# Cross-attention with a state-space scan on one core: pair-wise value products, projections in pieces, statistics and sums on ScalarE

## The chip, the core and the metric

The kernel runs on one core of one Trainium2 chip. The metric is the device time of one execution in microseconds; lower is better. The kernel before takes 2643.56 us, the median of 3 runs (2635.56 to 2644.17).

A core has five engines with a queue each, worked off in order: TensorE (PE: matmuls and transposes; its weight loads are shown as PEld), VectorE (DVE), ScalarE (ACT), GpSimd (POOL) and SyncE (SP), which here does nothing but issue transfers. An instruction that waits for another engine holds up all that is queued behind it.

## What is computed

The layer has 4096 queries of width 512 (`x`), 3202 keys and values that come from a second sequence, and 8 heads of 64. Cut to what matters here:

```python
xn   = layernorm(x, g1, beta1);  cn = layernorm(ctx, g1, beta1)
q    = xn @ Wq.T + bq;  k, v = cn @ Wk.T + bk, cn @ Wv.T + bv     # in 8 heads
attn = softmax(q @ k.T / 8)                                       # over 3202 keys
x1   = x + (attn @ v) @ W_o.T + b_o
U    = (layernorm(x1, g2, beta2) @ W_in.T + b_in) @ Bmat          # 4096 x 64
s_t  = silu(s_(t-1) @ A.T) + U_t                                  # a scan over the 4096 rows
out  = x1 + states @ Cmat + mod                                   # mod: one row, from ctxb
```

All of it is float32. The softmax takes a true maximum over the keys.

## The kernel before

**Stages.** A first stage (to 263 us of the profile) normalizes the 3202 rows of `ctx`, makes keys and values for all heads, parks them in DRAM (`kd`, `vd`), and makes the queries of the first chunk. The main loop (263 to some 2497 us) is the attention. A last stage projects the last chunk, runs the scan as three sweeps over 128-column blocks, and writes the output.

**The main loop.** The queries are cut into 8 *chunks* of 512 (`Q`). For each chunk the loop runs over 4 pairs of heads (`hp`) and 2 halves of 256 queries: that is a *unit*, 8 units to a chunk and 64 in all. A unit has 13 *steps*; a step handles two blocks of some 124 keys (so 2 heads x 2 key blocks x 256 queries, a tile of 123 x 1024). Each step of the loop carries five operations on tiles that belong to different steps of work, a software pipeline written out by hand (line 718, `manual_schedule`: what the program issues first stands first in each queue):

- `scores` (L453): four matmuls into the PSUM tile `s` (two such tiles exist), then the *copy* on ACT to SBUF (L469).
- `running` (L471), one step later: DVE takes the running maximum `top` from `s` (L480). The tile `s` is free again after this and the copy.
- `subtract` (L512), 16 steps after the scores: DVE takes the maximum off the copy (L514), in place.
- `weights` (L521), 17 steps after: ACT does the exponential in place (L524), POOL adds it to the sum `acc` (L533).
- `product` (L535), 18 steps after: four matmuls with the values into `po` (L542).

A `scores` matmul contracts 64 rows, a `product` matmul fills 64 output columns, all others use the whole 128 x 128 array.

**At the end of a unit** come the maximum over the keys (`maximum`, L482: eight transposes `tt` of `top`, two reductions on DVE, four transposes that spread the result, `mb`) and, after its last product, `finish` (L578: `both` on POOL, four transposes `pd`, a reduction `rd` and a reciprocal on DVE, the copy `wide` on ACT, two transposes `rb`, and the division on DVE, L613).

**Beside it** run two queues of generators, `first` (finish) and `rest`: `queries(Q + 1)` (L147) makes the next chunk's queries and `project(Q - 1)` (L616) takes the chunk before through the output projection `pa`, the second normalization, the transposes `tp` and the projection `pu` into `u`. `background` (L704) advances each by one `yield` at the end of a step, so after the copy of that step's scores in ACT's queue. A projection is issued whole: the 16 matmul passes of `pq` or the 8 of `pa` stand together.

**Transfers.** `load_k` and `load_v` (L674, L683) fetch keys and values once for both halves of a unit pair, into 13 buffers each. All main-loop transfers are in SP's queue: keys, values, the rows `x` for both generators, and the store of `x1` (L648), which waits for DVE's sum.

**The last chunk's projection** (L786) runs four generators in turn outside the hand-written order. Its PSUM tiles come from `ps_m` (2 banks), and its sum tile `x1` has one buffer. Between its operations POOL adds `modb` to 32 row tiles (`fetch`, L778).

Of the kernel before, what the change touches and what calls it, by code (L numbers as in the profile page):

```python
# [18 lines left out]
P = 128  # L19
# [26 lines left out]
def xattn_ssm_kernel(  # L46
# [58 lines left out]
    ln = actx.enter_context(tc.tile_pool(name="ln", bufs=2))  # L105
# [25 lines left out]

    def transposes(pool, tag, xh, n, name):

        tp = pool.tile([P, NC, P], F32, tag=tag, name=f"tp_{name}")
        for c in range(NC):
            nc.tensor.transpose(  # L136
                tp[:, c, :n], xh[:n, c * P : (c + 1) * P], ident[:n, :n]
            )
        return tp[:, :, :n]

    xp_ = actx.enter_context(tc.tile_pool(name="xp", bufs=2))
    xnp = actx.enter_context(tc.tile_pool(name="xnp", bufs=2))
    qp = actx.enter_context(tc.tile_pool(name="qp", bufs=6))
    ps_m = actx.enter_context(tc.tile_pool(name="ps_m", bufs=2, space=PSUM))
    qt = {}

    def queries(Q, fetched=None):  # L147

        xns = []
        for half in range(2):  # L150
            xn = xnp.tile([P, NC, QU], F32, tag="xn", name=f"xn_{Q}_{half}")
            xns.append(xn)
            for t in range(NT // 2):
                r = Q * QB + half * QU + t * P
                if fetched:
                    xt = fetched[:, half * (NT // 2) + t, :]
                else:
                    xt = xp_.tile([P, H], F32, tag="x", name=f"x_{r}", bufs=3)
                    nc.sync.dma_start(xt, x[r : r + P, :])
                    yield False  # L160
                scaled = normalize(xt, P, f"x{r}", later=True)
                yield False
                yield False
                xh = scaled()
                yield False
                tp = transposes(ps_m, "m", xh, P, f"x{r}")
                yield True
                nc.scalar.copy(xn[:, :, t * P : (t + 1) * P], tp)
                yield False
                yield False  # L170
        for hp in range(NC):
            pq = ps_m.tile([P, 512], F32, tag="m", name=f"pq_{Q}_{hp}")
            for half in range(2):
                for i in range(NC):
                    nc.tensor.matmul(  # L175
                        pq[:, half * QU : (half + 1) * QU],
                        wq[:, i, hp * P : (hp + 1) * P],
                        xns[half][:, i, :],
                        start=(i == 0),
                        stop=(i == NC - 1),  # L180
                    )
            yield True
# [5 lines left out]
            yield False  # L188
# [22 lines left out]
    def shift(k):  # L211

        pr = ps_m.tile([P, 512], F32, tag="m", name=f"pr_{k}")
# [9 lines left out]
        pb = ps_m.tile([P, 512], F32, tag="m", name=f"pb_{k}")  # L223
# [15 lines left out]
    def side():  # L239
# [30 lines left out]
        pw = ps_m.tile([P, 512], F32, tag="m", name="pw")  # L270
# [8 lines left out]
        pt = ps_m.tile([P, NC, P], F32, tag="m", name="pt")  # L279
# [12 lines left out]
        pb = ps_m.tile([P, 512], F32, tag="m", name="pb")  # L292
# [16 lines left out]
        pm = ps_m.tile([P, 512], F32, tag="m", name="pm")  # L309
# [11 lines left out]
        for dst, terms in (  # L321
# [3 lines left out]
            pr = ps_m.tile([P, 512], F32, tag="m", name="pr")  # L325
# [122 lines left out]
    sp_ = lctx.enter_context(tc.tile_pool(name="sp_", bufs=NDC + LAG + 4))  # L448
# [3 lines left out]
    def scores(w, c):  # L452
# [3 lines left out]
        for b in range(2):  # L456
            for a in range(2):
# [3 lines left out]
                    kts[(*w["at"][:2], c)][r, b * n : (b + 1) * n],  # L461
# [20 lines left out]
    def maximum(w):  # L482

        m = small.tile([P, 2, 2], F32, tag="m", name=f"m_{w['name']}")
        tps = []
        for t in range(2):
            tp = ps_m.tile([P, 2, 2, CK], F32, tag="m", name=f"tt_{w['name']}_{t}")
            tps.append(tp)
# [7 lines left out]
        yield  # L496
        for t in range(2):
            nc.vector.tensor_reduce(  # L498
                m[:, t, :], tps[t].rearrange("p a b k -> p a (b k)"), AX.X, ALU.max
            )  # L500
        yield
        mb = ps_b.tile([P, 2, QU], F32, tag="b", name=f"mb_{w['name']}")
        w["mb"] = mb
        for t in range(2):
            for a in range(2):
# [4 lines left out]
                )  # L510

# [456 lines left out]
```

## Time and profile before

| | |
|---|---|
| time, median of 3 runs | 2643.56 us |
| the profiled execution, its time | 2643.8 us |
| the profiled execution, its span | 2642.0 us |
| first stage | 0 to 263 us |
| main loop: first scores to last scores | 263.3 to 2465.4 us |
| last products, projection of the last chunk, scan | 2465.4 to 2642 us |

The span is what lies between the first and the last instruction; 1.8 us lie around it.

The timeline gives the start of every scores instruction. Each unit has 13 groups of them, so the start of each unit can be read off, and with it how long it lasts. The chunks 2 to 7 repeat one pattern to 0.4 us:

| unit of the chunk | 1 | 2 | 3 | 4 | 5 | 6 | 7 | 8 | sum |
|---|---|---|---|---|---|---|---|---|---|
| chunk 2 to 5, us | 30.9 | 34.8 | 38.2 | 36.0 | 32.3 | 32.7 | 44.9 | 30.9 | 280.8 |
| chunk 1, us | 24.3 | 27.8 | 30.9 | 32.8 | 32.7 | 44.9 | 30.9 | 30.9 | 255.3 |
| chunk 8, us | 30.9 | 34.8 | 38.2 | 36.0 | 30.8 | 30.9 | 30.9 | | |

Units 2 to 4 of a chunk carry `project`, units 5 and 6 the normalization in `queries`, unit 7 its four projections `pq`; units 1 and 8 have nothing beside them but `finish`. In chunk 1 there is nothing to project and `queries` comes a unit earlier.

In a line of the profile, a group such as `L480 DVE TENSOR_TENSOR top<-s,top` names line, engine, operation, and output and inputs. A timeline line gives start, duration, engine, line, operation, tiles, shape and count, and in brackets the idle time before it and what ended it. Neighbouring instructions of one engine overlap by some 0.05 to 0.1 us, so what one costs in a full queue is the distance from its start to the next start, not its duration.

### The profile page before, as it was taken

What the parts mean: (1) busy time and instruction counts of PE and PEld (TensorE: products, weight loads), DVE (VectorE), ACT (ScalarE), POOL (GpSimd) and SP (SyncE); (2) the same over time, 40 slices, a digit from 0 to 9 for tenths busy, and PEclk for the clock granted to TensorE, in tenths of its full rate; (3) what the DMA queues carried; (4) which work ended last, traced back from release to release, by engine and by line L of the source; (5) the groups of instructions that cost most, each with busy time, mean ns of one, the idle gap of its engine ahead of it and who ended that gap; (6) DMA issues with size and microseconds to landing.
All of it is one profiled execution on the core that took longest, in us unless ns stands there. A gap on an engine that the chain in (4) does not pass through costs nothing.

```text
span 2642.0 us, 44166 instructions
## 1 busy us (share of the span) xinstructions
PE 2498.9 (95%) x16588; PEld 1422.2 (54%) x16588; DVE 2144.1 (81%) x2320; ACT 1837.8 (70%) x2085; POOL 2066.3 (78%) x1170
## 2 busy tenths in 40 slices
PE   7989899999999999999999999999999999999857
PEld 3445456555565555555655555555655555555433
DVE  2210897999979897999799988999799979999725
ACT  2232787877878787878787777778787878788510
POOL 1020497998979997999799988989799979999860
PEclk9999999999999999999999999999999999999966
DMA  3422221112212121222112211222121312221133
GB/s 124 138 87 73 74 68 49 51 57 84 59 45 62 50 83 32 58 65 68 45 54 68 67 56 51 57 84 59 43 62 49 86 30 60 64 58 54 60 112 128
DMA packets 164458, 176.62 MB, mean 67 GB/s; under 512 B 13480, under 2 KB 137424, under 8 KB 164242
## 3 DMA queue, kind: packets, MB, share of 16 engines
q1 hardware_dynamic: 155070, 157.68, 20.6%
q10 hardware_dynamic: 9172, 16.06, 1.8%
q8 instruction: 134, 2.20, 0.4%
q14 instruction: 82, 0.67, 0.1%
HBM read 143.81 MB, written 29.89 MB: 66 GB/s over the span
## 4 chain that ended last, share of the span: by engine, by line
PE 50%; DVE 27%; issue 11%; ACT 7%; POOL 2%; DMA 1%; SPq 1%; ACTq 0%; DVEq 0%; POOLq 0%
DVE top L480 17%; PE s L459 14%; PE po L542 12%; DVE p L514 5%; PE pq L175 4%; ACT p L469 4%; PE pa L627 4%; PE pv L388 3%; PE pk L414 3%; ACT p L524 2%; PE tt L491 2%; PE py_c L870 1%; DVE rd L599 1%; PE mb L506 1%; PE pu L659 1%
## 5 line engine op out<-in xcount | busy, mean ns | idle before, releaser
L533 POOL TENSOR_TENSOR acc<-p,acc 123x1024 f32<-123x1024 f32 x698 | 1658.7, 2376 | 112.2 <-ACT p L524 70.6
L469 ACT COPY p<-s 123x1024 f32<-123x1024 f32 (+1 forms) x832 | 834.9, 1004 | 274.6 <-PE s L459 261.9
L514 DVE TENSOR_TENSOR p<-p,mb 123x1024 f32<-123x1024 f32 (+1 forms) x832 | 1000.0, 1209 | 0.8 <-PE mb L506 0.8
L459 PE MATMUL s<-q,k 64*123 64x256 f32 (+1 forms) x6656 | 941.4, 402 | 61.2 <-DVE top L480 49.4
L524 ACT ACTIVATE p<-p 123x1024 f32<-123x1024 f32 (+1 forms) x832 | 880.2, 1058 | 141.2 <-DVE p L514 134.0
L480 DVE TENSOR_TENSOR top<-s,top 123x1024 f32<-123x1024 f32 x704 | 855.9, 1216 | 140.1 <-ACT p L469 132.2
L542 PE MATMUL po<-p,v 123*64 123x256 f32 (+1 forms) x6656 | 900.4, 392 | 1.1 <-ACT o L585 0.9
L459 PEld LDWEIGHTS s<-q,k 64*123 64x123 f32 (+1 forms) x6656 | 560.2, 182 | 374.3 <-DVE top L480 169.3
L542 PEld LDWEIGHTS po<-p,v 123*64 123x64 f32 (+1 forms) x6656 | 404.4, 136 | 399.0 <-issue 222.5
L533 POOL TENSOR_TENSOR acc<-p,p 124x1024 f32<-124x1024 f32 x64 | 152.0, 2376 | 161.2 <-ACT p L524 161.0
L627 PE MATMUL pa<-wo,o 128*128 128x512 f32 x256 | 119.6, 612 | 2.5 <-DVE x L636 2.5
L115 POOL TENSOR_SCALAR ve_c<-mv_c 123x1 f32<-123x1 f32 (+1 forms) x26 | 5.9, 228 | 146.9 <-DVE mv_c L113 116.7
L175 PE MATMUL pq<-xn,wq 128*128 128x256 f32 x512 | 117.9, 383 | 0.0
L358 DVE COPY ct<-tp_c 128x492 f32<-128x492 f32 (+1 forms) x13 | 8.7, 671 | 127.8 <-PE tp_c L136 127.8
L480 DVE TENSOR_TENSOR top<-s,p 124x1024 f32<-124x1024 f32 x64 | 77.7, 1214 | 38.7 <-DMA k<-kd 37.4
L175 PEld LDWEIGHTS pq<-xn,wq 128*128 128x128 f32 x512 | 94.8, 190 | 20.5 <-issue 6.3
L388 PE MATMUL pv<-wv,ct 128*123 128x512 f32 (+1 forms) x208 | 97.8, 615 | 0.0
L422 ACT ACTIVATE ks<-pk,bias 128x492 f32<-128x492 f32 (+2 forms) x28 | 18.0, 643 | 111.8 <-PE pk L414 63.6
L414 PE MATMUL pk<-ct,wk 128*128 128x492 f32 (+2 forms) x224 | 89.2, 550 | 0.0
L588 POOL TENSOR_TENSOR both<-acc 124x512 f32<-124x512 f32 x63 | 80.8, 1283 | 4.9
L627 PEld LDWEIGHTS pa<-wo,o 128*128 128x128 f32 x256 | 46.8, 192 | 62.5 <-issue 56.5
L498 DVE TENSOR_REDUCE m<-tt 128x2 f32<-128x496 f32 x128 | 79.7, 662 | 0.7 <-PE tt L491 0.7
(158 smaller groups left out, 1345.5 us busy)
## 6 DMA issues: line engine op xcount, KB each, us to landing
k<-kd SPq DMA_DIRECT2D x352, 123.0 KB
v<-vd SPq DMA_DIRECT2D x352, 123.0 KB
xr<-in_x_dram SPq DMA_DIRECT2D x32, 256.0 KB
out_dram<-row_c ACTq DMA_DIRECT2D x32, 256.0 KB
k<-kd SPq DMA_DIRECT2D x64, 124.0 KB
v<-vd SPq DMA_DIRECT2D x64, 124.0 KB
x<-in_x_dram SPq DMA_DIRECT2D x28, 256.0 KB
x1d<-x SPq DMA_DIRECT2D x28, 256.0 KB
```

What stands on the lines that cost most here:

```text
L175: nc.tensor.matmul(pq[:, half * QU : (half + 1) * QU], wq[:, i, hp * P : (hp + 1) * P], xns[half][:, i, :], start=(i == 0), stop=(i == NC ...
L388: nc.tensor.matmul(pv[:n, :H], ct[:, i, o : o + n], wv[:, i, :], start=(i == 0), stop=(i == NC - 1),)
L414: nc.tensor.matmul(pk[:, :n_g], wk[:, i, hp * P : (hp + 1) * P], ct[:, i, :n_g], start=(i == 0), stop=(i == NC - 1),)
L459: nc.tensor.matmul(s[:n, a, b, :], kts[(*w["at"][:2], c)][r, b * n : (b + 1) * n], q[r], start=True, stop=True,)
L469: nc.scalar.copy(t[:n], s[:n])
L480: nc.vector.tensor_tensor(w["top"][:n], s[:n], before[:n], ALU.max)
L514: nc.vector.tensor_tensor(t[:n], t[:n], w["mb"][:n].unsqueeze(2).to_broadcast([n, 2, 2, QU]), ALU.subtract,)
L524: nc.scalar.activation(t[:n], t[:n], AF.Exp)
L533: nc.gpsimd.tensor_tensor(w["acc"][:n], t[:n], before[:n], ALU.add)
L542: nc.tensor.matmul(w["po"][a * HD : (a + 1) * HD, 0, :], vts[(*w["at"][:2], c)][:n, b, a * HD : (a + 1) * HD], t[:n, a, b, :], start=(c == ...
L588: nc.gpsimd.tensor_tensor(both, acc[:, :, 0, :], acc[:, :, 1, :], ALU.add)
L627: nc.tensor.matmul(pa, o_t[Q, c][:, t * P : (t + 1) * P], wo[:, c, :], start=(c == 0), stop=(c == NC - 1),)
```

## The change

The change keeps every result and shifts work between engines and within the step order:

- **Products by pairs.** At an odd step of a unit the products of this step and of the one before are issued together; at an even one none (the 13th stands alone).
- **Projections in pieces.** `pq` and `pa` are issued one matmul (of 512 columns) at a time, one per step. The two banks are split: `ps_m` for projections, `ps_f` for maxima and finish.
- **Maxima over two steps.** The transposes `tt` are issued in two halves at the ends of two steps, each followed by its reduction.
- **Statistics on ScalarE.** In the main loop `normalized` replaces the DVE statistics: a pass of ACT with a row sum, POOL's mean, a second pass of ACT (square) with a row sum, POOL's root, and the scaling as before.
- **Sums on ScalarE.** `rd` is made by four ACT instructions with a row sum; `u` is biased by ACT.
- **Order.** The "head" parts of the generators now stand in the step between `weights` and `scores` (before: after `scores`); the matmul parts ("pe") at its end, one per step, and none in the three steps after a unit's end. The projection runs as two generators `a` and `b`, two tiles each.
- **Keys and values per unit.** They are fetched for each half anew, into 6 and 9 buffers; `sp_` has one more.
- **The last chunk's projection** gets five banks of its own (`ps_t`), its matmuls alternate between the four tiles, and its emission order changes with the generator.

```diff
+    def normalized(xt, name, got):
+        xh = ln.tile([P, H], F32, tag="xh", name=f"xh_{name}")
+        total = ln.tile([P, 1], F32, tag="total", name=f"total_{name}")
+        nc.scalar.activation(xh, xt, AF.Identity, accum_out=total)
+        yield "head"
...
+        nc.gpsimd.tensor_scalar(mean, total, -1.0 / H, None, ALU.mult)
+        yield "head"
+        yield "head"
...
+        nc.scalar.activation(xh, xt, AF.Square, bias=mean, accum_out=square)
+        yield "head"
...
+        nc.gpsimd.tensor_scalar(ve, square, 1.0 / H, EPS, ALU.mult, ALU.add)
...
+        nc.gpsimd.tensor_tensor(rstd, ve, neg_half, ALU.pow)
...
+        nc.gpsimd.tensor_tensor(nmr, mean, rstd, ALU.mult)
+        yield "head"
+        yield "head"
+        nc.scalar.activation(xh, xt, AF.Identity, bias=nmr, scale=rstd)
+        got.append(xh)
...
-    ps_m = actx.enter_context(tc.tile_pool(name="ps_m", bufs=2, space=PSUM))
+    ps_m = actx.enter_context(tc.tile_pool(name="ps_m", bufs=1, space=PSUM))
+    ps_f = actx.enter_context(tc.tile_pool(name="ps_f", bufs=1, space=PSUM))
...
+            for i in range(NC):
+                nc.tensor.matmul(
+                    pq,
+                    wq[:, i, hp * P : (hp + 1) * P],
+                    xn[:, i, :],
...
+                if i < NC - 1 and not fetched:
+                    yield "pe"
+            yield "head"
...
-    sp_ = lctx.enter_context(tc.tile_pool(name="sp_", bufs=NDC + LAG + 4))
+    sp_ = lctx.enter_context(tc.tile_pool(name="sp_", bufs=NDC + LAG + 5))
...
         for t in range(2):
-            tp = ps_m.tile([P, 2, 2, CK], F32, tag="m", name=f"tt_{w['name']}_{t}")
-            tps.append(tp)
+            tp = ps_f.tile([P, 2, 2, CK], F32, tag="m", name=f"tt_{w['name']}_{t}")
...
-        yield
-        for t in range(2):
+            yield
             nc.vector.tensor_reduce(
...
-        nc.vector.tensor_reduce(rd, pd, AX.X, ALU.add)
...
+        for t in range(2):
+            for a in range(2):
+                nc.scalar.activation(
+                    junk, pd[:, t, a, :], AF.Identity, accum_out=rd[:, t, a : a + 1]
+                )
+        yield "head"
         nc.vector.reciprocal(rd, rd)
         nc.scalar.copy(wide, rd.unsqueeze(3).to_broadcast([P, 2, 2, HD]))
...
             for c in range(NC):
                 nc.tensor.matmul(
                     pa,
...
+                if c < NC - 1:
+                    yield "pe"
+            yield "head"
             x1 = xp.tile([P, H], F32, tag="x1", name=f"x1_{r}")
             nc.vector.tensor_tensor(x1, pa, xt, ALU.add)
...
+                got = []
+                yield "head"
+                nc.sync.dma_start(x1d[r : r + P, :], x1)
+                yield from normalized(x1, f"y{r}", got)
...
-            nc.vector.tensor_scalar(
+            nc.scalar.activation(
                 u[hs, :, c0 : c0 + P // L].rearrange("s j c -> s c j"),
...
-        if half == 0:
-            t = kp.tile([P, 2 * CK], F32, tag="k", name=f"k_{Q}_{hp}_{c}")
+        t = kp.tile([P, 2 * CK], F32, tag="k", name=f"k_{i}_{c}", bufs=AHEAD + 2)
...
+        t = kp.tile([CK, 2, P], F32, tag="v", name=f"v_{i}_{c}", bufs=AHEAD + 5)
...
+    beside = {"finish": [], "a": [], "b": [], "queries": []}
...
+    def heads():
+        for k in beside:
+            if advance(k, "head") and owner == [k]:
+                owner.clear()
+
+    def tail():
+
+        if advance("finish", "pe"):
+            return
+        for k in owner or ("a", "b", "queries"):
+            if advance(k, "pe"):
+                owner[:] = [k]
+                break
...
             if prev:
                 running(*prev)
+            for k in (2, 3):
+                if k in ends:
+                    next(ends[k]["max"])
             if exp:
                 weights(*exp)
+            heads()
             if now:
                 scores(*now)
...
-                product(*mul)
+
+                w, c = mul
+                for k in (c - 1, c) if c % 2 else (c,) if c == NDC - 1 else ():
+                    product(w, k)
...
-            background(more=1 not in ends)
...
+            if not ends:
+                tail()
...
-    tails = [project(NQB - 1, (t,), (tp_, NT, NT)) for t in range(NT)]
+    lastx = ExitStack()
+    ps_t = lastx.enter_context(tc.tile_pool(name="ps_t", bufs=5, space=PSUM))
+    tails = [project(NQB - 1, (t,), (tp_, NT, NT, ps_t)) for t in range(NT)]
```

## The prediction

> **What bounds the kernel now.** I read the stages first, then the timeline of a light unit and of a heavy one, then groups, waits and the tail. 83% of the span is the main loop, so the stretch from 340 to 2480 us comes first:
>
> ```profile
> core 0: us, PE busy (x) PEld busy (x) DVE busy (x) ACT busy (x) POOL busy (x), PEclk, DMA share, GB/s
> 340.00:2480.00 2140.00, 2086.36 (x15018) 1210.44 (x15014) 1971.02 (x2017) 1688.65 (x1863) 1925.08 (x998) 1.00 0.20 58
> ```
>
> The reader is to see that three engines are above 89%, that ACT has 451 us free, that the granted clock is 1.00 throughout and that the transfers use a fifth of their engines. None of them bounds the loop alone, so each unit must be summed. I take pitches (start to next start) from stretches without gaps:
>
> ```profile
> 880.70 1.13 PE L459 MATMUL s<-q,k 64*123 64x256 f32 x8
> 881.76 1.08 PE L542 MATMUL po<-p,v 124*64 124x256 f32 x8
> 882.78 0.66 PE L136 MATMUL tp_y<-ident,xh_y 128*128 128x128 f32 x4
> 883.36 0.91 PE L459 MATMUL s<-q,k 64*123 64x256 f32 x6
> ```
>
> Scores cost PE 1.06, products 1.015, `tp` .585; read likewise, `tt` .996, `mb` and `pd` .57 each, `rb` .37, `pu` .97, a `pq` block 3.65 and a `pa` block 3.63. DVE: `top` 1.135, subtraction 1.128, `m` .58, `rd` .70, the reciprocal .10, division .33, `bn_stats` with its second step .81, `x1` .725, `u` .275. A unit has 12 `top`s and 13 subtractions, so DVE needs 12x1.135 + 13x1.128 + 2x.58 + .70 + .10 + .33 = 30.6; PE needs 29.5 in a light unit (1 and 8 of a chunk), and such a unit lasts 30.9. Over the eight units PE's sums are 29.5 34.7 38.3 36.2 30.7 30.7 44.1 29.5 (273.6). The larger of PE's and DVE's sum gives every unit within .9 us. So light units, and 5 and 6, are DVE's; 2, 3, 4 and 7 are PE's.
>
> What matters most for this change is how tight the loop is in a light unit:
>
> ```profile
> 2434.33 1.21 DVE L514 TENSOR_TENSOR p<-p,mb 123x1024 f32<-123x1024 f32 x1
> 2435.46 1.22 DVE L480 TENSOR_TENSOR top<-s,top 123x1024 f32<-123x1024 f32 x1
> 2435.57 1.06 ACT L524 ACTIVATE p<-p 123x1024 f32<-123x1024 f32 x1 [0.30 <-DVE p L514]
> 2436.54 0.99 ACT L469 COPY p<-s 123x1024 f32<-123x1024 f32 x1
> 2437.72 1.22 DVE L480 TENSOR_TENSOR top<-s,top 123x1024 f32<-123x1024 f32 x1
> ```
>
> The exponential starts .03 after its subtraction ends, the copy follows at 2436.54 and ends at 2437.53, and `top` of the same scores starts .19 later. In all 768 pairs of the trace `top` never starts before the copy ends (least distance .03 us). So there is a ring: subtraction 1.2, exponential .96, copy 1.0, then `top`; anything put into ACT between exponential and copy beyond .19 us holds DVE up. Today the small ACT work stands behind the copy, where the next exponential has .30 us to wait anyway.
>
> **What the change removes and adds, part by part.**
>
> *Products by pairs.* Going from scores to products costs PE more than staying: two product blocks in one run, from the end of the loop, show it.
>
> ```profile
> 2487.34 1.90 PE L542 MATMUL po<-p,v 123*64 123x256 f32 x16
> 2489.07 1.03 PE L558 MATMUL pd<-p,ones 123*64 123x256 f32 x8
> ```
>
> 1.73 for two, against 2.03. A unit has six pairs and so saves six switches of about .15: .9 per unit, 7.3 per chunk; two scores that come to stand together save another .1, 1 per chunk. This is PE time, worth something only in PE's units. A pair delays the next scores by .85; the second tile of `s` takes that up.
>
> *Pieces.* A piece is two passes of .429 and one switch of .197: 1.055. Four make 4.22 against 3.63: +.59; eight blocks per chunk: +4.7. What it removes is the hole of a whole block:
>
> ```profile
> 734.64 1.23 DVE L480 TENSOR_TENSOR top<-s,top 123x1024 f32<-123x1024 f32 x1 [3.39 <-ACT p L469]
> ...
> 734.93 3.62 PE L175 MATMUL pq<-xn,wq 128*128 128x256 f32 x16
> ```
>
> DVE stood for 3.39 us around such blocks. But in units 2 to 4 and 7 PE has no gap there, so closing DVE's hole alone gives nothing; the gain comes from moving: `pq` now falls on units 7 and 8 with two blocks each, so PE has 37.0 + 37.0 where it had 44.1 + 29.5, and unit 8 no longer idles PE. The two units lasted 75.8 and should last 74.2: −1.6.
>
> The Trainium skill ("Perfetto Trace Analysis", Optimizing Tensor Performance, on matmuls) says that larger matmuls are more efficient than smaller ones. By that alone the pieces would just cost their 4.7 us per chunk; the row of the 3.39 us hole says that a block costs its neighbours as well.
>
> *Maxima.* `tt` in two halves: one more switch, +.17 per unit, 1.3 per chunk on PE. PE's sums thereby become 28.4 33.8 36.0 36.5 32.3 29.6 37.0 37.0 = 270.6, −3.0 per chunk.
>
> *Statistics.* DVE loses .81 for each of 8 tiles per chunk, 6.5 us, mostly in units 1 to 5. ACT gains two passes of 128x512 per tile. The scaling beside them has a pitch of .72; with a row sum I bound each by .72 and 1.06 (the exponential with twice the columns) and take .75, the nearest row. All three now stand between exponential and copy, so each loses .56 net of the .19 where DVE or ACT sets the pace. POOL gets `mean` (.3) per tile: 262 us per chunk, below every estimate of a chunk here.
>
> *Sums.* `rd` leaves DVE (−.70 per unit: 29.9) for four ACT instructions on 128x124, all in one step. The nearest rows: a copy of 128x128 from PSUM by ACT is .28, `wide` .40. Four are 1.1 to 2.0 with the writes to one scratch tile in turn; I take 1.5, of which 1.3 is lost after the slack. `wide` then waits for a reciprocal that stands behind other DVE work: +.2. The biased `u` is .3 on ACT, .1 lost; it takes .275 from DVE.
>
> The Trainium skill ("ScalarE: Activation LUTs", Rules for kernel authors) puts plain arithmetic on VectorE, not on ScalarE. Its formula in the section on what ACT_TABLE_LOAD costs (186 ns and .833 ns per element) makes four times 289 ns, 1.16 us, an estimate; the light unit would be .3 shorter by it, 31.4. It speaks against this part either way, and the row that bears on it is `rd` at .70 on DVE for all four sums.
>
> *Light unit after:* 29.9 + .3 (as now, 30.9 against 30.6) + 1.3 + .2 = **31.7** (31.3 to 32.2 by the bounds of `rd`), against 30.9. So a unit of the kind that DVE binds gets .8 longer although DVE has less to do.
>
> *Heavy units.* For each I set PE's sum beside the ring (30.2 + 1.5 + .56 per pass + `x1` .725 + .3 to .4 per `xn` or `q`). Passes per unit, from the built order: 0 1 9 5 5 4 0 0.
> Unit 2: PE 33.8, ring 33.0; only four steps carry a piece and the others fall back to the ring's pace, so 34.8. Unit 3: PE 36.0, ring 38.7; several passes share a step and pay the slack in the shadow of a piece: middle, 37.5. Unit 4: 36.5 and 34.9: 36.9. Unit 5: 32.3 and 35.5: 34.6. Unit 6: 29.6 and 34.5: 33.9. Units 7 and 8: 37.0 and 32.5: 37.1.
> Sum 31.7 34.8 37.5 36.9 34.6 33.9 37.1 37.1 = **283.6** against 280.8: +2.8 per chunk.
>
> *Keys and values per unit.* 416 more transfers of each kind and smaller rings. SP needs .3 per issue and a transfer lands some 2.5 us later (first scores: 2.53 on `k`); keys are asked for 4 steps ahead, 9 us or more. Share of the transfer engines .20 becomes some .37. Behind the `x1` store, which waits on SP for DVE (28 times, 345 us in sum, 17.4 at most), keys can be late:
>
> ```profile
> SPq L688 <- PE po L542: 1137.2, 354, 29.0
> SPq L648 <- DVE x L636: 344.7, 28, 17.4
> ```
>
> The store is issued one `yield` after `x1` now, so its wait shrinks. I take 0; without that cover it costs the landing time, 2.5 per store.
>
> *Tail.* Its rows stand between the statistics of the tiles:
>
> ```profile
> 2508.92 0.22 POOL L115 TENSOR_SCALAR ve_y<-mv_y 128x1 f32<-128x1 f32 x1
> ...
> 2510.19 0.81 ACT L125 ACTIVATE xh_y<-x,nmr_y,rstd_y 128x512 f32<-128x512 f32 x1 [12.76 <-POOL nmr_y L119]
> ```
>
> In the built order ten row additions of 1.23 precede the first `ve` on POOL (one before), and alternating the matmuls makes the first tile's `pa` end some 7.5 later, the last tile's no later. Bounds: −6 (the five banks take 2 us per tile out) to +11 (nine additions in full); I take +6.
>
> *Sum.* Six chunks (2 to 7) x 2.8 = +17; chunk 1 has pieces and `rd` but no projection: +3; chunk 8 has light units only at its end, four x .8: +3; tail +6. In all +29 on the profiled execution's 2643.8 (span 2642.0 and 1.8 around it; .2 from the median): 2673.
>
> **The rivals.**
> *Faster: ACT's insertions hide.* If an engine may run ahead between units, the ring's loss comes off DVE's saved time, and a unit is the larger of PE and DVE: 30.2 33.8 36.0 36.5 32.3 30.2 37.0 37.0 = 273.0, −7.8 per chunk; −47 over six, −2 in the rest, +6 in the tail: 2601. Half of the loss hidden: 2637. For it: ACT's 451 free us. Against: the .19 in the timeline above and no case in 768 that got round it. Chance .26 for anything below 2636.
> *No change:* gains and losses within .3% (8 us, about what a measurement can tell from no change): .13.
> *Slower by more: ACT and POOL in series.* A pass that waits for POOL's `mean` or root, which stands behind an `acc` of 2.46, stops the copy behind it. Eight tiles with two such waits; a wait in full costs up to 2.4, a half of them at 1.2 each is +10 per chunk on six: 2673 + 40 beyond what is covered, 2713. It decides from a second where POOL is more than two steps behind. For: POOL at 90%. Against: two steps lie between. Chance .13.
> *SP starves PE:* 28 stores, behind each a key and a value tile late by the 2.5 of a landing, none of it regained: 28 x 2 x 2.5 = +140, 2813. It decides once a store holds SP for more than the lead of 4 steps. Against: 17.4 at most today, with keys issued early enough that scores waited only for DVE. .03.
> *Forecast:* 2650 to 2700, .45.
>
> **How the numbers follow.** Slower is .45 + .13 + .03 = .61, same .13, faster .26. The range goes down to 2618, between the half and the full gain, and up to 2712.
>
> **What would show it.** Right: light units of 31 to 32 with DVE idle before `top`, released by the copy, in the step with the four `rd` instructions; units 7 and 8 at some 37; PE's sum some 3 less per chunk; the first `ve` of the tail later. Wrong: light units at 30.2; `pq` units with PE idle; a queue of SP waiting on the store while `s` waits for `k`.

## The result, and the profile after

The changed kernel takes 2727.31 us, the median of 6 runs (2719.97 to 2735.46), against 2643.33 before (6 runs): ratio **1.0331**, 95% interval 1.0307 to 1.0354. It is slower, as forecast, but by 84 us and not by 29, and outside the range. The profiled execution took 2733.4 us (span 2731.4). Against the profile before it gained these lengths:

| stretch | before, us | after, us | difference | forecast |
|---|---|---|---|---|
| first stage, to the first scores | 263.3 | 268.7 | +5.4 | 0 |
| chunk 1 | 255.3 | 268.8 | +13.5 | +3 |
| chunks 2 to 7 | 1685.6 | 1744.6 | +59.0 | +17 |
| chunk 8, to the last scores | 261.2 | 271.3 | +10.1 | +3 |
| what follows | 176.6 | 178.0 | +1.4 | +6 |

The same window query as before, over the loop of the changed kernel:

```profile
core 0: us, PE busy (x) PEld busy (x) DVE busy (x) ACT busy (x) POOL busy (x), PEclk, DMA share, GB/s
340.00:2540.00 2200.00, 2079.92 (x14698) 1186.85 (x14700) 1879.30 (x1799) 1842.28 (x2588) 1909.04 (x1045) 0.99 0.35 102
```

VectorE has less to do in a longer stretch, and ScalarE is nearly as full as it. No engine is busier than PE was before. In one chunk (1080 to 1361 us before, 1121 to 1411 after) PE, VectorE and GpSimd stand idle longer than before; only ScalarE stands less (46.8 us in place of 60.2). VectorE's waits in that chunk (columns: the waiting line, what released it, us in all, times, longest). Before:

```profile
DVE top L480 <- ACT p L469: 18.2, 15, 3.8
```

After (L515 is `top`, L504 the copy, L557 the exponential, L637 the four sums, L642 `wide`, L695 `xn`, L701 `pu`):

```profile
DVE top L515 <- ACT p L504: 40.7, 50, 1.6
DVE m L530 <- PE tt L524: 2.5, 4, 1.0
```

Few long waits, most of them behind the blocks of `pq`, have given way to 50 shorter ones. The kernel before also had 4.2 us behind `pa` and `xr`, which are gone; so VectorE waits 20.8 us more per chunk, and does 13.2 less (8 x .70, 8 x .81, 4 x .275). That is 7.6 of the 9.2 by which a chunk became longer. Each wait of `top`, those under .15 us included, can be sorted by what stood just ahead of its copy. In 21.0 us the copy itself had waited, for late scores all but .9 (17.5 before); 19.9 stood behind a small operation of ScalarE (none before, where the other 1.6 stood behind the exponential alone): 6.2 of it with the four sums last, 1.3 with `wide`, 9.7 with one of the three passes of the normalizations.

One place in unit 5, from the timeline, shows how one delay is handed on:

```profile
1284.74 1.06 ACT L557 ACTIVATE p<-p 123x1024 f32<-123x1024 f32 x1
1285.70 0.26 ACT L637 ACTIVATE wide<-pd 128x124 f32<-128x124 f32 x1
1285.85 0.20 ACT L637 ACTIVATION_READ_ACCUMULATOR wide<-pd 128x1 f32 x1
...
1287.04 0.19 ACT L637 ACTIVATION_READ_ACCUMULATOR wide<-pd 128x1 f32 x1
1287.13 0.62 ACT L136 ACTIVATE xh_x<-x 128x512 f32<-128x512 f32 x1
...
1287.75 1.00 ACT L504 COPY p<-s 123x1024 f32<-123x1024 f32 x1
...
1288.78 1.22 DVE L515 TENSOR_TENSOR top<-s,top 123x1024 f32<-123x1024 f32 x1 [1.56 <-ACT p L504]
...
1290.17 0.40 ACT L642 COPY wide<-rd 128x256 f32<-128x256 f32 x1 [0.47 <-DVE rd L641]
1290.48 0.58 ACT L695 COPY xn<-tp_y 128x512 f32<-128x512 f32 x1
...
1291.12 1.73 PE L701 MATMUL pu<-xn,wc 128*64 128x128 f32 x8 [2.67 <-ACT xn L695]
...
1292.01 1.22 DVE L515 TENSOR_TENSOR top<-s,top 123x1024 f32<-123x1024 f32 x1 [0.81 <-ACT p L504]
```

Exponential, then four sums (1285.70 to 1287.13: 1.43 us), then a pass over `x` (.62), and only then the copy: `top` waits 1.56. One step on, `wide` waits for a reciprocal that stands behind the late `top`, `xn` stands behind `wide`, the copy behind both, and `top` loses .81 more. PE, which stood for 2.67 us before `pu`, then runs at half clock for 3.4 us. The first line below has the columns of the window query (the granted clock is the .50); the second is the next scores; the two after them are the same place in e10, which has no such wait:

```profile
1291.41:1294.81 3.40, 3.40 (x18) 2.23 (x16) 2.35 (x2) 1.95 (x3) 2.71 (x3) 0.50 0.08 27
1292.77 2.07 PE L494 MATMUL s<-q,k 64*123 64x256 f32 x8
...
1267.18 1.09 PE L696 MATMUL pu<-xn,wc 128*64 128x128 f32 x8 [1.45 <-ACT xn L690]
1268.19 1.13 PE L494 MATMUL s<-q,k 64*123 64x256 f32 x8
```

Such a dip stands in unit 5 of each of the chunks 2 to 7, and in no chunk of the kernel before after its first unit.

### The profile page after: what moved, and what is told of

Read it like the earlier page. It is cut to its first block, busy times and chain, and to the rows that moved or that the text cites. A ratio compares the mean times of both kernels' runs of the same rounds, so it can differ in the third digit from the quotient of the medians.

```text
span 2731.4 us, 46342 instructions
## 1 busy us (share of the span) xinstructions
PE 2500.9 (92%) x16332; PEld 1400.1 (51%) x16332; DVE 2063.9 (76%) x2113; ACT 2008.7 (74%) x2845; POOL 2067.0 (76%) x1226
## 4 chain that ended last, share of the span: by engine, by line
PE 55%; DVE 18%; ACT 14%; issue 5%; POOL 5%; DMA 2%; SPq 1%; ACTq 0%; POOLq 0%; DVEq 0%
PE s L494 18%; PE po L575 16%; DVE top L515 10%; DVE p L547 6%; ACT p L504 6%; PE pq L209 5%; PE pv L423 3%; POOL acc L566 3%; PE pa L667 3%; ACT p L557 3%; PE pk L449 2%; ACT wide L637 2%; DVE m L530 1%; PE tt L524 1%; PE py_c L930 1%
## 5 line engine op out<-in xcount | busy, mean ns | idle before, releaser
L515 DVE TENSOR_TENSOR top<-s,top 123x1024 f32<-123x1024 f32 x704 | 859.9, 1221 | 313.7 <-ACT p L504 310.9
L504 ACT COPY p<-s 123x1024 f32<-123x1024 f32 (+1 forms) x832 | 836.9, 1006 | 205.3 <-PE s L494 189.8
L557 ACT ACTIVATE p<-p 123x1024 f32<-123x1024 f32 (+1 forms) x832 | 881.6, 1060 | 134.2 <-DVE p L547 131.8
L575 PE MATMUL po<-p,v 123*64 123x256 f32 (+1 forms) x6656 | 824.7, 389 | 0.5 <-ACT o L618 0.5
L494 PEld LDWEIGHTS s<-q,k 64*123 64x123 f32 (+1 forms) x6656 | 566.8, 184 | 438.4 <-issue 178.6
L575 PEld LDWEIGHTS po<-p,v 123*64 123x64 f32 (+1 forms) x6656 | 441.1, 137 | 331.3 <-issue 118.3
L209 PE MATMUL pq<-xn,wq 128*128 128x512 f32 x256 | 140.6, 638 | 1.2 <-ACT xn L203 1.2
L667 PE MATMUL pa<-wo,o 128*128 128x512 f32 x256 | 140.1, 638 | 0.0
L515 DVE TENSOR_TENSOR top<-s,p 124x1024 f32<-124x1024 f32 x64 | 77.8, 1216 | 36.1 <-ACT p L504 36.1
L524 PE MATMUL tt<-ident,top 124*128 124x124 f32 x512 | 82.2, 283 | 21.6 <-DVE top L515 21.6
L530 DVE TENSOR_REDUCE m<-tt 128x2 f32<-128x496 f32 x128 | 85.2, 666 | 18.2 <-PE tt L524 18.2
L524 PEld LDWEIGHTS tt<-ident,top 124*128 124x128 f32 x512 | 52.7, 140 | 69.7 <-DVE top L515 36.8
```

The costliest lines, as they stand in the source:

```text
L209: nc.tensor.matmul(pq, wq[:, i, hp * P : (hp + 1) * P], xn[:, i, :], start=(i == 0), stop=(i == NC - 1),)
L494: nc.tensor.matmul(s[:n, a, b, :], kts[w["i"], c][r, b * n : (b + 1) * n], q[r], start=True, stop=True,)
L504: nc.scalar.copy(t[:n], s[:n])
L515: nc.vector.tensor_tensor(w["top"][:n], s[:n], before[:n], ALU.max)
L524: nc.tensor.transpose(tp[:, a, b, :], w["top"][:, a, b, t * P : (t + 1) * P], ident[:CK, :CK],)
L557: nc.scalar.activation(t[:n], t[:n], AF.Exp)
```

## The experiments

"Chunk" is the length of chunk 4 or 5. "Light" is the seventh unit of the last chunk, which has only `finish` beside it: a unit of that kind that follows a unit which PE binds reads up to 1.2 shorter, since scores start late there. Each kernel was run beside the kernel before on the same chip; a time without a ratio is one execution.

| kernel | units 1 to 8, us | chunk | light |
|---|---|---|---|
| before | 30.9 34.8 38.2 36.0 32.3 32.7 44.9 30.9 | 280.8 | 30.9 |
| forecast | 31.7 34.8 37.5 36.9 34.6 33.9 37.1 37.1 | 283.6 | 31.7 |
| changed | 31.6 35.6 38.5 36.5 37.2 35.4 38.0 37.2 | 290.0 | 32.8 |
| e1 all small operations behind | 30.8 35.8 41.8 38.4 39.5 36.0 37.2 37.3 | 297.0 | 31.9 |
| e2 sums and statistics on VectorE | 30.8 35.6 36.9 36.5 34.0 34.1 38.0 37.2 | 283.1 | 32.0 |
| e3 both | 30.8 35.8 38.3 37.9 38.6 35.0 37.2 37.3 | 291.0 | 31.8 |
| e4 no pairs | 31.7 35.3 38.0 37.4 34.9 34.5 38.1 38.1 | 288.0 | 32.1 |
| e5 = e2, whole blocks | 32.0 38.4 42.6 34.5 34.3 45.4 32.0 32.0 | 291.2 | 32.0 |
| e6 = e2, no pairs | 30.9 35.3 37.0 37.4 34.1 33.4 38.1 38.1 | 284.3 | 31.3 |
| e9 = e2, whole, no pairs | 31.3 37.8 41.5 35.1 33.5 44.7 31.3 31.3 | 286.5 | 31.3 |
| e10 four sums on VectorE | 30.8 35.6 37.2 36.5 34.0 34.7 38.0 37.2 | 284.1 | 32.0 |
| e13 `finish` behind | 30.7 35.6 37.6 36.5 34.2 34.2 38.0 37.2 | 284.1 | 31.9 |

**e1 to e4: place, amount, order of PE.**

e1, and e3:

```diff
-            heads()
             if now:
                 scores(*now)
             if 3 not in ends and sub:
                 subtract(*sub)
+            heads()
```

e2, and e3:

```diff
-        for t in range(2):
-            for a in range(2):
-                nc.scalar.activation(
-                    junk, pd[:, t, a, :], AF.Identity, accum_out=rd[:, t, a : a + 1]
-                )
+        nc.vector.tensor_reduce(rd, pd, AX.X, ALU.add)
...
-        nc.scalar.activation(xh, xt, AF.Identity, accum_out=total)
-        nc.scalar.activation(xh, xt, AF.Square, bias=mean, accum_out=square)
+        nc.vector.bn_stats(st, xt)
+        nc.vector.bn_aggr(mv, st)
```

e4:

```diff
-                for k in (c - 1, c) if c % 2 else (c,) if c == NDC - 1 else ():
-                    product(w, k)
+                product(w, c)
```

> The small operations of the generators are issued behind the scores and the second subtraction again, as before the change; all else as in the changed kernel, whose chunks 4 to 7 last 290.0 us (before: 280.8). Theory A (place): what matters is that ScalarE's small work stands between the exponential and the copy, where .19 us is free, and not behind the copy, where .30 more is free; some 45 of the 64 insertions of a chunk stand where the ring sets the pace, so some 8 to 14 us per chunk come back: chunk 276 to 282, light unit 30.9, about 2640 us in all. Rival B (amount): ScalarE's four sums and two passes hold the loop up wherever they stand: chunk 287 to 290. Rival C (PE's order): the pairs and pieces make scores late, since half of VectorE's 41 us of waiting per chunk stands behind late scores: chunk 287 to 290 too, with VectorE's wait behind late scores still some 20 us.

Measured 2769.44 us: 42 slower than the changed kernel. Theory A holds in units 1 and light ones (−.8, −.9), and fails in units 3 to 5 (+3.3, +1.9, +2.3). PE's waits in one chunk:

```profile
PE tp_x L160 <- ACT u L705: 4.8, 2, 3.3
PE s L494 <- DVE top L515: 4.7, 8, 1.6
PE pu L701 <- ACT xn L695: 4.2, 3, 3.3
```

With the small operations behind the copy, `xn` and `u` come later (PE waits 4.2 and 4.8 us for them, 2.7 and 2.3 in the changed kernel), while the matmuls that read or replace them stand at the end of the same step; all projections share one PSUM bank. VectorE's waits behind copies that had themselves waited rise from 21.0 to 34.2 (2.7 of it for GpSimd). Each chunk also has three dips to half clock, in units 3, 5 and 6. So the place ahead of the scores seems to serve these operations and to be wrong for others; no run tells apart how much is the waits for `xn` and `u` and how much the dips.

> The sums of finish and the statistics of the main loop are VectorE's again, at the same places in the order; the rest as in the changed kernel (chunk 290.0). Theory A: the copy's delays by the four sums and the two passes (6.2 and 6.7 us of VectorE's waiting per chunk) go, VectorE gets 12 us of work back; light unit 31.2, units 3, 5 and 6 shorter by some 1 each, chunk 285 to 289. Rival B (amount): ScalarE is what holds the loop up; chunk 278 to 282, light unit 30.9. Rival C: 289 to 291.

2678.7 us: 6.9 off a chunk, three quarters of what the change had cost there. The execution is still 39 us above that of the kernel before beside it (2639.5).

> Both edits together: sums and statistics on VectorE, small operations behind the scores; what is left of the change is pairs, pieces, maxima in halves, transfers per unit. Theory A: the ring is as free as before, so a unit is the larger of PE's sum and VectorE's (30.9 33.8 36.0 36.5 32.3 30.9 37.0 37.0): chunk 274 to 277, some 2600 us in all, faster than before the change. Rival C: VectorE still waits some 15 us or more per chunk for late scores in units that PE's sum doesn't bind; chunk 281 to 286.

2728.68 us. It falls short of both: moving the small operations back costs 8 us per chunk again (29.7 of waiting behind late copies, 24.2 of it for scores and 5.1 for GpSimd). Its chunks have no dip, one or two in these units, and so price one: unit 3 lasts 39.9 with a dip and 38.3 without, unit 5 38.6 and 37.0.

> A product at every step again, the rest as in the changed kernel (chunk 290.0). Rival C (the pair delays the next scores by .85 us): units 2, 3, 5 and 6 become shorter by 1 to 2 although PE has .9 more to do in each, VectorE's waiting behind late scores falls from 21 us to under 12 per chunk; chunk 285 to 289. Theories A and B: PE has 7.3 us more per chunk, units 4, 7 and 8 longer by .9 each, the others as they are: chunk 292 to 295.

2708.7 us, −2.0 per chunk, unit 5 alone −2.3 and unit 4 +.9, as theory C said in kind; the waits behind late scores fell only to 16.2. Unit 5 has no dip here, and by e3's price of 1.6 for one that is the larger part of its −2.3.

**e5, e6, e9: pieces and pairs as a square.** Edits: whole blocks (the `yield "pe"` between the matmuls of `pq` and `pa` left out), e4's edit, and both, each on e2.

> As e2 (sums and statistics on VectorE; chunk 283.2, units 30.8 35.6 36.9 36.5 34.0 34.1 38.0 37.2), and the projections in whole blocks again. Theory P (pieces are a price): PE gets .59 per block back and the projection of a tile holds its PSUM bank for a shorter time; units 7 and 8 fall to some 36.5 and 36.0, unit 2 to 35.2, chunk 279 to 282. Rival H (pieces pay for themselves): each whole block opens a hole of 3.4 us in VectorE's work that the next steps make up only in part; units 2 to 4 longer by .5 to 1.5 each, chunk 284 to 288.

2727.95 us. Neither number: the blocks go at once where pieces had waited their turn, so unit 6 holds all of `pq`, and units 2 and 3 hold two blocks of `pa` each.

> As e2 (chunk 283.2), and a product at every step again. From e4, where it took 2.0 us off a chunk of the changed kernel, mostly in units 5 (-2.3) and 6 (-.9), while units 4 and 8 gained .9: theory C (a pair makes the next scores late by .85) says units 5 and 6 fall to 32.5 and 33.3 here too and units 4, 7, 8 gain up to .9: chunk 281 to 283. Rival B2 (those units were late because of ScalarE's passes, which are gone here, not because of the pairs): units 5 and 6 stay at 34, PE's 7.3 more show: chunk 285 to 288.

2680.59 us. Units 5 and 6 hardly move (+.1 and −.7), so it was mostly ScalarE's work, and the dip in unit 5 that comes with it, that made the pairs harmful there; chunk +1.1.

> Sums and statistics on VectorE, whole blocks and a product at every step: what is left of the change is the order of the small operations, one bank for projections, maxima in halves, transfers per unit. It closes a square: pieces with pairs 283.2 (e2), pieces without pairs 284.3 (e6), whole blocks with pairs 291.2 (e5), and the kernel before, which has neither, 280.8. If pairs and pieces are all that matters beside ScalarE's sums, this is 280 to 282, with light units of 31.0 and a unit 6 of 44 to 45 that holds the four blocks. If the one bank and the order of the small operations cost by themselves: 284 to 288, with units 2 and 3 together over 75 (before: 73.0).

2687.55 us. With neither pieces nor pairs the chunk is 286.5, still 5.7 above before, nearly all of it in units 2 to 4 (114.4 against 109.0). The new order puts a `pa` block of unit 4 into unit 2; how much of the 5.4 is this, and how much one bank or the maxima in halves, is not told apart. Pieces and pairs together take 3.3 of it back; pairs alone add 4.7, pieces alone take off 2.2.

**e7, e8: one part of the change on the kernel before.**

e7 has the changed kernel's loop over `(c - 1, c)` in place of `product(*mul)`. e8, in `queries`:

```diff
             qt[Q, hp] = t
             yield False
+            if hp == 1 and not fetched:
+                for k in range(12):
+                    yield False
```

> The kernel before (chunk 280.8; units 30.9 34.8 38.2 36.0 32.3 32.7 44.9 30.9) with nothing of the change but the products by pairs; as many buffers as before. If the pairs save PE's switches where PE binds: units 2, 3, 4 and 7 shorter by .9 each, the others by 0 to +.3: chunk 277 to 278, some 2615 to 2622 us, ratio .990 to .993. Theory C (the pair delays the scores that follow it, and what PE saves is lost where VectorE binds): units 1, 5, 6, 8 longer by .5 to 1 each, chunk 279.5 to 282, ratio .997 to 1.005.

Ratio 1.0079 (1.0062 to 1.0096), chunk 283.1 to 285.2 (the longest has two dips to half clock): slower, though PE's busy time fell from 274.6 to 267.4 us per chunk. Light units lose .7, nearly all at one place, after a unit's end. In e7, and then in the kernel before:

```profile
1126.89 1.13 PE L459 MATMUL s<-q,k 64*124 64x256 f32 x8
1127.95 1.95 PE L542 MATMUL po<-p,v 123*64 123x256 f32 x16
1129.83 1.13 PE L459 MATMUL s<-q,k 64*123 64x256 f32 x8
1130.31 1.21 DVE L480 TENSOR_TENSOR top<-s,p 124x1024 f32<-124x1024 f32 x1
1130.89 0.65 PE L506 MATMUL mb<-ident,m 128*124 128x128 f32 x4
1131.06 1.01 ACT L469 COPY p<-s 123x1024 f32<-123x1024 f32 x1 [0.97 <-PE s L459]
...
2439.99 1.13 PE L459 MATMUL s<-q,k 64*124 64x256 f32 x8
2442.06 1.13 PE L459 MATMUL s<-q,k 64*123 64x256 f32 x8
```

The second scores start 2.94 after the first, where before they started 2.07 after them, and their copy waits .97 for them. `mb` comes no later (4.00 after the first scores; 4.15 before): it is the scores behind the pair that are late, and VectorE stands .58 for their copy between two `top`s.

> The kernel before with nothing of the change but the place of the projections of the queries: two whole blocks in unit 7, two in unit 8. PE's sums of these units become 36.8 and 36.8 in place of 44.1 and 29.5, both above VectorE's 30.6: if a unit is the larger of the two sums, they last 37.1 each, 74.2 in place of 75.8, a chunk 279.2, some 2631 us, ratio .994 to .996. Rival H: four blocks' holes at other places cost as much as the idle PE of unit 8 gives: 75.5 to 77, ratio .999 to 1.003.

Ratio .9986 (.9977 to .9996), chunk 281.0: no gain. Units 7 and 8 last 38.0 each, 76.0 for 75.8. So a block of 3.65 costs the unit it stands in 3.5, wherever it is ((44.9 − 30.9)/4, and (38.0 − 30.9)/2): the PE time that a light unit leaves idle, .19 per step by the prediction's pitches (1.135 + 1.128 − 1.06 − 1.015), can't be saved up for it.

**e10, e11, e12: the sums alone, a pair's place, the transfers.** Edits: e2's first part on the changed kernel; on e2, `(c,) if c in (8, 9, NDC - 1)`; on e6, no loads in a pair's second unit, with fewer buffers elsewhere to make room.

> The changed kernel (chunk 290.0) with the four sums of finish back on VectorE, the statistics still on ScalarE. e2 gave 6.8 us per chunk for both. VectorE's waits put 6.2 us per chunk on the four sums and 6.7 on the two passes, and VectorE takes back .70 x 8 = 5.6 and .81 x 8 = 6.5. If the four sums are the costlier part, since they stand in every unit: 284.5 to 286.5. If the passes are: 288 to 290, with light units still .8 shorter (e2's 32.0 in place of 32.8 in the last chunk) and units 3 and 5 as they are (38.5 and 37.2).

2687.6 us. The four sums are nearly all: −5.9 per chunk, unit 5 −3.2, unit 3 −1.3, light units −.8. The dip in unit 5 is gone with them. The statistics are worth the .9 to 1.0 that remains to e2.

> As e2 (chunk 283.2, light unit of the last chunk 32.0), with the pair that falls into the second step after a unit's end issued one by one. Theory E (a pair costs only there, since the scores that it makes late are those whose maximum stands ahead of the next subtraction): light units of the last chunk 31.0 to 31.3, units 2, 5 and 6 shorter by .3 to .7, chunk 281 to 282.5. Rival (a pair costs everywhere that VectorE binds): light units 31.8 to 32, chunk 283 to 283.5.

2724.46 us, chunk 288.4: both readings missed. Light units stayed at 32.0, and five others gained .9 to 1.1. With a product ahead of the first `tt`, the two reductions come later, and PE waits for them:

```profile
PE mb L536 <- DVE m L528: 5.8, 8, 1.0
```

In e2 that wait is not among PE's. The changed kernel keeps this step free of products; by this run it needs to.

> As e6 (chunk 284.3, clock .979, 2680 us), with keys and values fetched once for two units again; to have the room, one buffer less for the weights (as before the change) and one less for the normalization's tiles. If the added transfers cost nothing but perhaps clock: chunk 284 to 284.6, the granted clock without its dips to .91 in the loop (.982), 2672 to 2680 us. If they delay anything: chunk under 283.

2672.68 us, chunk 284.4: with the transfers of the kernel before and fewer buffers the repeated chunks are as they were, so the added transfers seem to delay nothing there. The 8 us lie in the first stage and chunk 1 (5.2) and at the end, with the clock at .985 against .979; whether by the transfers or by the buffers that were changed too stays open.

**e13 to e15: place of the sums alone.**

e13, and e15:

```diff
-            heads()
+            heads(("a", "b", "queries"))
             if now:
                 scores(*now)
             if 3 not in ends and sub:
                 subtract(*sub)
+            heads(("finish",))
```

e14, and e15:

```diff
             nc.scalar.copy(xn, tp)
+            yield "head"
             yield "pe"
```

> The changed kernel (chunk 290.0; units 31.6 35.6 38.5 36.5 37.2 35.4 38.0 37.2; light units of the last chunk 32.8) with the small operations of finish alone behind the scores and the second subtraction; those of the projections and queries stay ahead of the scores. Theory A (place): with .49 us free there in place of .19 the four sums lose less: light units 32.0 (e1 gave 31.9 with all behind), chunk 283 to 287, without e1's longer units 3 to 5 (41.8 38.4 39.5). Theory W (the sums hold up xn and the copy alike wherever they stand): light units 32.0 too, but unit 5 stays at 36.5 to 37.5, chunk 288 to 290. Amount alone: no unit moves by over .3.

2684.93 us, chunk 284.1, equal to e10. The same four instructions on the same engine, one place further on, with the rest of `finish`, cost nothing more than on VectorE; unit 5 falls to 34.2, without its dip. So it was mostly the place, not the amount. `wide`, the reciprocal and the division moved with the sums; what the sums alone gain by it is not told apart. Theory W, which had unit 5 stay at 36.5 to 37.5, falls.

> The changed kernel with one more step between the copy xn and the projection pu of each tile; nothing else. Theory W: PE's waits for xn (2.7 us per chunk, in unit 5) go, unit 5 falls from 37.2 to 35 to 36, chunk 288 to 289. If PE's wait is covered anyway by VectorE's work: unit 5 within .3 of 37.2 and the chunk within .5 of 290.0.

2743.04 us, chunk 291.8 to 292.0. PE's wait for `xn` is gone, and units 5 and 6 last 76.5 in place of 72.6. But the added step moved other work: 6 of the 16 pieces of `pq` now stand in unit 6 and only 2 in unit 8, and two pieces of `pa` went from unit 4 to unit 5. Units 5 to 8 together last 147.2 and 148.3 (147.8 in the changed kernel), so the run doesn't price the wait for `xn` alone.

> Both edits. If A and W are separate causes the gains add: chunk 281 to 286. If one covers the other, as the better of the two alone, within .5.

2701.3 us, chunk 285.8: worse than e13 alone.

**e16 to e18: the sums in the kernel before, behind the copy.**

`rd` is made by the changed kernel's four activations, and between them and the reciprocal stands

```diff
+        yield False
         nc.vector.reciprocal(rd, rd)
```

once in e16 and e17, twice in e18. e17 has the changed kernel's `u` too.

> The kernel before (chunk 280.8, light unit 30.9) with the four sums of finish on ScalarE, behind the copy, where its small operations stand; one step between them and the reciprocal. If the place is all that matters, VectorE's .70 per unit is worth up to .2 in light units (GpSimd's own sum is 30.7) and .5 in units 5 and 6: chunk 279.3 to 280.2, ratio .994 to .998, faster than both kernels. If the sums cost by their amount, or GpSimd or ScalarE binds as well: 280.6 to 283, ratio .999 to 1.008.

> As e16, with the bias of u on ScalarE too: VectorE saves a further .275 in units 2 to 5 each, which counts only in unit 5. Place: chunk .1 to .5 below e16. Else: equal to it or up to .5 above.

Ratios 1.0176 (1.0150 to 1.0203) and 1.0142 (1.0122 to 1.0161), chunks 286.4 and 285.9. VectorE's waits in e16:

```profile
DVE top L480 <- ACT p L469: 18.1, 16, 3.8
DVE rd L607 <- ACT wide L603: 11.1, 8, 1.8
```

A matmul step in the generator makes the next call advance twice, so the one `yield` put no step between sums and reciprocal: VectorE stood 1.4 us for them in every unit.

> As e16 (chunk 286.4, light unit 31.5; before 280.8 and 30.9), with the reciprocal a step after the sums. If e16's loss was VectorE's wait for the sums (11.1 us per chunk at the reciprocal): that wait is gone, light unit 30.7, units 5 and 6 .3 to .5 shorter than before, chunk 279 to 280.5, ratio .993 to .999. If the sums cost by themselves: light unit 31.2 or more, ratio over 1.005.

Ratio 1.0017 (1.0002 to 1.0032), chunk 281.2:

```profile
DVE top L480 <- ACT p L469: 24.3, 25, 3.8
```

The wait at the reciprocal is gone, and `top` waits 6.1 us more per chunk behind ScalarE's later copies (3.9 of its waits now come from a copy that waited for GpSimd's `acc`): what VectorE saves (5.6) it waits away. No version tried beats the kernel before by anything but e8's .14%, which its chunks don't show.

## Why the prediction was right and wrong

**Right: the sign, and the mechanism of a part of it.** Work between exponential and copy holds up VectorE, and e13 shows that the place decides for the operations of `finish`. The four sums' +.8 in a light unit is what e10 and e13 give (32.8 against 32.0 and 31.9); that unit 1 lasts 31.6, as forecast, is by chance, since it follows a unit that PE binds. Four sums at 1.5 and passes at .75 measured 1.43 and .62 to .72. The place of the pieces, 37 us in units 7 and 8, was about right (38.0, 37.2). But the sign didn't hang on this mechanism alone: without any of ScalarE's new work (e2) the chunk is still 2.3 longer than before, where the forecast had a gain.

**Wrong, and the larger miss: a unit as the larger of two sums.** This rule gave the units before within .9, but not for the right reason. By it the change without ScalarE's new work should bring a chunk to 274.4 (30.9 33.8 36.0 36.5 32.3 30.9 37.0 37.0, the sum expected for e3); e2 measured 283.1. These 8.7 are more than the 6.4 by which the whole chunk was missed. The work on ScalarE, 9.2 of the forecast from there on (283.6 − 274.4), measured 6.9: too little for the four sums, too much for the passes, whose statistics cost .9. What binds, as e8, e6 and e7 show, is each step. A block costs 3.5 in any unit; a piece costs .85 in e6 ((38.1 − 31.3)/8), its 1.055 less about the .19 that a step leaves. So spreading `pq` could bring nothing: units 7 and 8 were forecast at 74.2 and last 75.2. Likewise the pairs' .9 of PE time came back only in units 4 and 8. The words "the second tile of `s` takes that up" failed there: a light unit loses .7 by the pairs (e7; e2 against e6), and in the changed kernel they cost 2.0 per chunk (e4), the dip in unit 5 included. The order, the single bank and the halves, put at hardly anything but 1.3 of PE time, are the 5.7 of e9; which of them costs it stays open.

**Wrong: the loss of the four sums in heavy units.** The step that failed is in "Sums": "1.3 is lost after the slack", +.2 for `wide`, and then in "Heavy units" half of it let off where "several passes share a step". Charged that way (.8 net in each of the units 1, 3, 5 and 6) the sums make a chunk some 3 longer than with VectorE's reduction; e10 measured 5.9. The missing part is in units 3 and 5 (1.3 and 3.2 for some .8 each): there the sums stand in one step with a pass, nothing is free for either, and `wide`, `xn` or `u`, and the next copy queue behind the late reciprocal. Sharing a step made it worse, where the forecast had made it better. In unit 5 the clock adds to it: the late `xn` leaves PE idle for 2.67 us, and the dip to half clock follows. Where the same unit of one kernel has a dip in one chunk and none in another, it is 1.3 to 1.6 longer (e3; e7's unit 5, 34.3 and 33.0). By that estimate 1.3 to 1.6 of unit 5's 3.2 is the dip, a term that the forecast didn't have.

**Mis-sized: the ends.** Chunks 1 and 8 were charged with the sums alone; they carry pairs, passes and one bank as well. The first stage was left out; there PE waits 12.4 us for `xh_x` where it waited 5.0 (and 3.9 for `xh_c`, which are gone). The tail's +6 was +1.4. Its sign came: the first `ve` stands 56.3 us behind the last scores, 43.5 before, with ten row additions ahead of it; but the tail as a whole regained nearly all of that. "PE's sum some 3 less per chunk" did not come: PE is busy for 275.4 us, .8 more than before, with a dip in it, and in e2, without one, for 273.5, only 1.1 less.

**The rivals.** Hiding behind ScalarE's free time fell (e18: even in the better place nothing is gained). POOL's series did not come: the passes' statistics cost .9 in all, and POOL is busy for 251.2 us of a chunk (put at 262). SP did not starve PE: the store's wait shrank, as was said, and in the whole execution PE waited for `k` twice, 4.4 us in all (3.9 before).

```profile
SPq L689 <- DVE x L678: 66.0, 28, 3.0
```

Transfers, taken as free, seem to be free in the loop (e12).

In the parts that the runs do tell, a chunk's +9.2 is: four sums +5.9 (e10, the dip in unit 5 included), statistics +.9 (e2 to e10), order, bank and halves +5.7 (e9, not told apart), pieces and pairs −3.3 (e9 to e2).

## What to carry to other kernels

Before moving work to a less busy engine, find the ring that runs through that engine and ask how much may be put at the exact place in its queue; a share of 79% says nothing of it. Here, with two tiles of run-ahead, a unit cost about the sum over its steps of the slowest engine (e6 to e8), so neither spreading a block nor saving time on an engine in steps that it doesn't bind brought anything. When two kernels are compared unit by unit, see first whether the same work and the same granted clock stand in the unit. The same edit can help or hurt with its neighbours: the pairs cost 4.7 us with whole blocks and bring 1.1 with pieces.

## What the runs showed of the hardware

An activation with a row sum appears as two records, the pass and a read of the accumulator: .26 and .20 us on 128 x 124, .38 to .40 from one sum to the next, .26 from the last to another operation. On 128 x 512 it mostly took .62 to .72 to the next start, no more than the scaling without a sum (.70 to .72). The Trainium skill ("ScalarE: Activation LUTs", What ACT_TABLE_LOAD costs) gives a pass by its elements, an estimate of 1.16 us for the four sums one after the other; 1.43 was measured; the read of the accumulator, .20 each, is not in that figure. Its rule that plain arithmetic belongs on VectorE (Rules for kernel authors) agrees with .70 there, but e10 and e13, with the same chunk of 284.1, show that here it made no difference once the place was right.

The granted clock of the changed kernel's loop dips to half for 3.4 us at a time; ten windows of 20 us read .91 for it between 340 and 2540 us. From 340 us to its last scores the kernel before has none, and PE is never idle there for more than .98 us at once; e2 has none either. In the chunks 2 to 7 the dip in unit 5 begins within 1.1 us of the end of PE's wait of 2.6 to 2.7 us. The wait's length alone doesn't decide: PE's idle times of 2.3 to 2.4 us in unit 3 of the chunks 3 to 7 bring none, and in e15 dips follow idle times of 1.1 us. What decides is not shown.
